# Router products in a shared buffer rotation, and the preparation steps of the second feed-forward spread over more products

## The chip, the cores and the metric

The kernel runs on one core of one Trainium2 chip, in one launch. The metric is the device time of that launch in microseconds (us); lower is better. Engines are named as in the profile: PE is TensorE's matmul, PEld its weight load, DVE is VectorE, ACT is ScalarE, POOL is GpSimd, SP is SyncE, whose queue (SPq) issues most DMAs. L670 is line 670 of the kernel.

## The reference

Two layers over x of shape (8, 512, 512), each with a gated cross-attention and a gated feed-forward. The change touches only the last of the four stages:

```python
# x: (8, 512, 512); ctx: (8, 64, 512); 32 experts, 8 groups, inner width 192
x = x + tanh(g_xattn[0]) * linear_attention(layernorm(x), ctx, ...)      # "xa0"
x = x + tanh(g_ffn[0])   * gelu_mlp(layernorm(x), ...)                   # "ff0", width 2048
x = x + tanh(g_xattn[1]) * masked_softmax_attention(layernorm(x), ctx)   # "xa1"
x = x + tanh(g_ffn[1])   * merged_moe(layernorm(x), ...)                 # "ff1"

def merged_moe(h):
    probs = softmax(h @ gate_weight.T)                  # (token, 32)
    top_val, top_idx = top_k(probs, 8)
    top_val = top_val / sum(top_val)
    w = sum over k of top_val[k] * onehot(merge_groups[top_idx[k]], 8)   # (token, 8 groups)
    gate, up = split(h @ gate_up[dominant_experts])     # 8 groups x 192 each
    y = (silu(gate) * up) @ down[dominant_experts]
    return sum over groups of w * y
```

All is float32, and all eight groups are computed for every token, weighted by w.

## The kernel before, in words

A batch of 512 tokens is the unit of the outer loops: eight batches go through the first attention, then eight through the first feed-forward (ff0), then eight through the second (ff1). Every big matrix product is done by a scheme of seven half-size products instead of eight; a "product" below is one of these seven. A product of an up projection (class Up, L754) is four matmuls of 128x128 by 256 columns, which the profile counts as eight.

In ff1 a batch has six up units (Ff1Up, in the order 1, 0, 3, 2, 5, 4) and one down projection (SplitDown, L941). The products of a unit come in the order 1, 2, 6, 5, 7, 4, 3, those of the down in the order 2, 4, 1, 6, 5, 7, 3. The last two products of an up unit, and the last of the down, are held back and issued after the first product of the next unit. So the end of a batch's 49 products reads: last unit's 2, 6, 5, 7 (38th to 41st), down 2 (42nd), last unit's 4 and 3 (43rd, 44th), down 4, 1, 6, 5, 7 (45th to 49th). SplitDown splits each of its products a second time in seven; for that `combine` (L928 to L931) forms four sums of 128x384 on DVE ("split2", "split4" and so on, two buffers in rotation) before the product that takes them.

After an up product ACT copies the result out of PSUM (u1, u6, u7, L766), DVE adds two results (g L833, up L847), ACT takes the tanh (th, L836), and DVE multiplies by the token's share of the group (L837, L839) and by the other half (a, L843 and L851). The buffers u, g, th and up are all drawn from one rotation of eight tiles of 2 KB a partition (`temp`, L121).

Beside the products of batch n runs the preparation of batch n + 1, a generator (`prep_ff1`). Each of its steps is taken after some product of the plan. In ff1 it is: second attention (transposes pt, scores pst, psc, softmax, pe, pr), layer norm and transposes again, router logits (plt, pl), the largest 8 of 32 (L657, L658), their scaling (L663), and then for each of four blocks of 128 tokens a product by group on POOL (wg_e, 128x256, L670) and a sum over experts on DVE (w, L673). Then w is transposed on PE (pw, L677), copied (wT), written to DRAM ("shares", L680, ACT's queue), and read back in five broadcast DMAs on SP's queue into the tiles "share" of the first two units (`spread_share`, L695). Last come the four token sums S (L539 to L542). The loop over the plan deals out the steps evenly: `count` steps over `until` products; the last piece (S) is taken at a given product of the down.

What sets the order: in the attention and ff0 the order on some engines is that of the code. From the first batch of ff1 on (`in_order.clear()`) no engine is held to it, and a scheduler orders each engine's instructions by the place at which the code issues them and by its own idea of when operands are ready. Each engine then executes its own queue in that order, and an instruction that waits holds all behind it. SP's queue also loads the weights, in tiles of 256 KB into a ring of 16 tiles, in the order in which the products use them.

Of the kernel before, what the change touches and what calls it, by code (L numbers as in the profile page):

```python
# [21 lines left out]
F32 = mybir.dt.float32  # L22
# [8 lines left out]
P = 128  # L31
B, S, D = 8, 512, 512
# [6 lines left out]
E, G, I = 32, 8, 192  # L39
# [29 lines left out]
def flamingo_kernel(  # L69
# [39 lines left out]
    def psum(name):  # L109
        return bank["ps"].tile([P, 512], F32, tag="ps", name=name)  # L110
# [10 lines left out]
    def temp(name):  # L121
        return work.tile([P, 512], F32, tag="t2", name=name, bufs=8)
# [406 lines left out]
    def prep_xa0(b):  # L529
        xnT = yield from normed("xa0", b, f"xa0_{b}")  # L530
        yield "last"
        blocks["xa0", b] = xnT, token_combinations("xa0", b, xnT)

    def token_combinations(ph, b, xnT):

        s = work.tile([P, 4, 2, H2], F32, tag="S", name=f"S_{ph}_{b}", bufs=1)
        a11, a12 = xnT[:, 0:2, 0:H2], xnT[:, 2:4, 0:H2]
        a21, a22 = xnT[:, 0:2, H2:S], xnT[:, 2:4, H2:S]
        nc.vector.tensor_tensor(s[:, 0], a21, a22, ALU.add)  # L539
        nc.vector.tensor_tensor(s[:, 1], s[:, 0], a11, ALU.subtract)  # L540
        nc.vector.tensor_tensor(s[:, 2], a11, a21, ALU.subtract)
        nc.vector.tensor_tensor(s[:, 3], a12, s[:, 1], ALU.subtract)  # L542
        return s

    def prep_ff0(b):
        xnT = yield from normed("ff0", b, f"ff0_{b}")

        xb = xs["ff0", b]
        for t in range(NT):
            nc.gpsimd.tensor_tensor(xb[:, t, :], xb[:, t, :], b2_sb, ALU.add)  # L550
        yield "last"
        blocks["ff0", b] = xnT, token_combinations("ff0", b, xnT)
# [74 lines left out]
    def prep_ff1(b):  # L627
        yield from cross_attention(b)
        xnT = yield from normed("ff1", b, f"ff1_{b}")

        plt = psum(f"plt_{b}")[:, 0:P]
        for c in range(NC):
            for t in range(NT):
                nc.tensor.matmul(
                    plt[ts(t, E), :],
                    lhsT=router_sb[:, c, :],
                    rhs=xnT[:, c, ts(t, P)],
                    start=c == 0,
                    stop=c == NC - 1,
                )  # L640
        lT = hpool.tile([P, P], F32, tag="lT", name=f"lT_{b}", bufs=1)
        nc.scalar.copy(lT, plt)
        yield
        pl = psum(f"pl_{b}")[:, 0 : NT * E]
        nc.tensor.transpose(pl, lT, ident)
        pl = pl.rearrange("p (t e) -> p t e", e=E)
        top = small.tile([P, NT], F32, tag="rtop", name=f"rtop_{b}")
        nc.vector.tensor_reduce(top, pl, AX.X, ALU.max, negate=True)

        pr = hpool.tile([P, NT, E], F32, tag="router", name=f"router_{b}", bufs=1)  # L650
        for t in range(NT):
            nc.scalar.activation(pr[:, t, :], pl[:, t, :], AF.Exp, bias=top[:, t : t + 1])
        yield
        best = small.tile([P, NT, 8], F32, tag="best", name=f"best_{b}")
        rest = hpool.tile([P, NT, E], F32, tag="rest", name=f"rest_{b}", bufs=1)
        for t in range(NT):
            nc.vector.max(best[:, t, :], pr[:, t, :])  # L657
            nc.vector.match_replace(rest[:, t, :], best[:, t, :], pr[:, t, :], 0.0)  # L658
        total = small.tile([P, NT], F32, tag="rtotal", name=f"rtotal_{b}")
        nc.vector.tensor_reduce(total, best, AX.X, ALU.add)  # L660
        nc.vector.reciprocal(total, total)
        nc.vector.tensor_tensor(pr, pr, rest, ALU.subtract)
        nc.vector.tensor_tensor(pr, pr, total.unsqueeze(2).to_broadcast([P, NT, E]), ALU.mult)  # L663

        wg_e = hpool.tile([P, G, E], F32, tag="wg_e", name=f"wg_e_{b}")
        w = small.tile([P, G, NT], F32, tag="w", name=f"w_{b}")
        for t in range(NT):
            if t:
                wg_e = hpool.tile([P, G, E], F32, tag="wg_e", name=f"wg_e_{b}_{t}")
            nc.gpsimd.tensor_tensor(  # L670
                wg_e, of_group, pr[:, t, :].unsqueeze(1).to_broadcast([P, G, E]), ALU.mult
            )
            nc.vector.tensor_reduce(w[:, :, t], wg_e, AX.X, ALU.add)  # L673
        for _ in range(4 if b == 0 else 2):
            yield
        pw = psum(f"pw_{b}")[0 : G * NT, 0:P]
        nc.tensor.transpose(pw, w.rearrange("p g t -> p (g t)"), ident)  # L677
        wT = hpool.tile([G * NT, P], F32, tag="wT", name=f"wT_{b}", bufs=1)
        nc.scalar.copy(wT, pw)
        nc.scalar.dma_start(out=shares[b], in_=wT)  # L680
        yield
        for i in FF1_UNITS[0:2]:
            spread_share(b, i)
        yield "last"
        blocks["ff1", b] = xnT, token_combinations("ff1", b, xnT)
# [3 lines left out]
    def spread_share(b, i):  # L689

        t = hpool.tile([P, 2, S], F32, tag="share", name=f"share_{b}_{i}", bufs=3)
        rows = shares[b].rearrange("(g t) q -> g (t q)", t=NT)
        for n in range(2):
            for g, lo, hi in pieces(P * (2 * i + n), P * (2 * i + n + 1), P):
                nc.sync.dma_start(  # L695
                    out=t[lo % P : (hi - 1) % P + 1, n, :],
                    in_=rows[g : g + 1, :].partition_broadcast(hi - lo),
                )
        spread_of[b, i] = t
# [305 lines left out]
    class QUp(Up):  # L1005
        ph, i = "xa0", 0
# [116 lines left out]
    def steps(units, late=late):  # L1123
# [9 lines left out]
    work_list = (  # L1133
        [("xa0", b, prep_xa0(b)) for b in range(B)]
        + [("ff0", b, prep_ff0(b)) for b in range(B)]
        + [("ff1", b, prep_ff1(b)) for b in range(B)]
    )

# [70 lines left out]
    for b in range(B):  # L1209
# [15 lines left out]
        g = GUp(b)  # L1225
# [50 lines left out]
    plan = []  # L1276
# [29 lines left out]
    down_of = {u.b: u for u, _, _ in plan if isinstance(u, SplitDown)}  # L1306

    def tiles_of(u, m):

        if isinstance(u, SplitDown):  # L1310
            n, of = SPLIT_ORDER.index(m), 7 * SPLIT_CHUNKS
            return -(-of * 7 // 4) - of * 6 // 4 if n == 6 else of * (n + 1) // 4 - of * n // 4
        return 1 if u.kind == "up" else u.chunks // 2
# [15 lines left out]
    hpool = stack(tc.tile_pool(name="inner", bufs=1, reuse_waits="tile"))  # L1329
# [31 lines left out]

    def steps_of(ph, b, _):

        return 5 if ph == "ff0" else 22 if b else 24

    at, held = None, False
    for u, m, n in plan:
        if n != at:
            if n == 2 * B:
                in_order.clear()  # L1370
            if at is not None and n < 3 * B:
                for _ in work_list[n][2]:
                    pass
            at, k, held = n, 0, False
        if n == 2 * B and k == 0:
            for _ in builder:
                pass
            build.close()
            second = stack(tc.tile_pool(name="second", bufs=1, reuse_waits="tile"))
        u.step(m)  # L1380
        for _ in range(tiles_of(u, m)):
            next(loads, None)
        for _ in range(4):
            if pending:
                pending.pop(0)()
        if isinstance(u, Ff1Up) and u.i == FF1_UNITS[-1]:

            if m == 2:
                down_of[u.b].combine(2)
                down_of[u.b].combine(4)  # L1390
            if m == 3:
                down_of[u.b].combine(1)
        if isinstance(u, SplitDown) and m in (4, 1, 6, 5, 7):
            u.combine(SPLIT_ORDER[SPLIT_ORDER.index(m) + 1])
        k += 1
        if k == 6:
            flush()
        if u.kind == "up" and u.ph == "ff1" and m == 5 and u.i < 4:
            spread_share(u.b, FF1_UNITS[FF1_UNITS.index(u.i) + 2])
        if k % 4 == 0:  # L1400
            next(builder, None)
        if n + 1 == 3 * B:
            continue
        if n == B + 2 and k == 10:
            groups()
        if k == 20 and n + 2 < 3 * B:
            load_x(*work_list[n + 2][0:2])
        prep = work_list[n + 1][2]
        if held:
            if u.kind == "down" and u.b == work_list[n][1] and m == u.order[1]:  # L1410
                for _ in prep:
                    pass
            continue

        until = sum(p == n for _, _, p in plan) - 6
        count = steps_of(*work_list[n + 1])
        if k * count // until > (k - 1) * count // until:
            held = next(prep, None) == "last"
# [47 lines left out]
```

## Time and profile before

| | us |
|---|---|
| median of 3 runs | 2149.47 (2148.35 to 2151.68) |
| the profiled execution | 2149.74 |
| its span | 2147.9 |
| PE waits for w before pw | 15.5 in 6 waits |
| POOL waits for w before wg_e | 15.8 in 24 waits |
| wg_e on POOL, 128x256, median | 0.727 (0.722 to 1.039), 32 of them |
| w on DVE, median | 0.421, 32 of them |
| a sum of 128x384 for the down (L928 to L931) | 0.55 |
| an elementwise 128x512 on DVE (L839) | 0.69 |

The span is the profiled execution from its first to its last instruction; its own time includes what lies around that. Durations of single instructions are those of the profile's rows; a start-to-start distance is the time that an engine was really taken up, because matmuls overlap at their ends. The batches of ff1 follow each other at 118 to 120 us in the chain of work that ended last (the down's product 4 starts at 1290.1, 1408.5, 1528.6, 1648.1, 1766.3, 1886.3, 2006.1 and 2111.5), and the last of them, with no preparation beside it, takes 105.4.

### The profile page before, as it was taken

Reading aid. Unit: us, or ns where it says so; the run is one execution under the profiler, and the core shown is the slowest. Engines: PE = TensorE matmul, PEld = TensorE weight load, DVE = VectorE, ACT = ScalarE, POOL = GpSimd, SP = SyncE. Lnnn points to the kernel's source line nnn. Section 1 sums busy time; section 2 is a strip of 40 time slices with the busy share of each in tenths; the row PEclk is TensorE's granted clock in tenths of the full one; section 3 lists DMA queues with packets and bytes.
Section 4 is the critical chain, followed back from the end, with each engine's and each line's share of the span. In section 5 each row is a group of like instructions: output and inputs, shape, how many; then the busy total and the mean of one; then the engine's idle time right before and its main releaser. Section 6 shows DMA issues by size and latency. Waiting matters only on the chain.

```text
span 2147.9 us, 30849 instructions
## 1 busy us (share of the span) xinstructions
PE 2096.3 (98%) x11452; PEld 1810.3 (84%) x11452; DVE 1241.4 (58%) x2289; ACT 557.4 (26%) x1146; POOL 251.7 (12%) x228
## 2 busy tenths in 40 slices
PE   8999999999999999999999999999999999999998
PEld 4778787788888888888888889898888889888988
DVE  3687787542333324232434377777777777776757
ACT  3433333212130303121233221312122222213121
POOL 2121111321111120030200010000000000000000
PEclk8999999999999999999999999999999999999999
DMA  7345634677676765666747658586776758585865
GB/s 221 118 152 168 198 120 111 219 243 226 203 232 181 241 205 168 200 213 189 229 156 251 193 167 284 180 265 198 233 229 199 250 169 282 166 263 158 251 205 166
DMA packets 258453, 434.84 MB, mean 202 GB/s; under 512 B 34304, under 2 KB 75936, under 8 KB 254208
## 3 DMA queue, kind: packets, MB, share of 16 engines
q1 hardware_dynamic: 250864, 406.10, 61.0%
q10 hardware_dynamic: 5856, 23.20, 2.9%
q0 software_dynamic: 1584, 3.57, 0.7%
q8 instruction: 92, 1.51, 0.3%
q14 instruction: 57, 0.47, 0.1%
HBM read 369.00 MB, written 63.77 MB: 201 GB/s over the span
## 4 chain that ended last, share of the span: by engine, by line
PE 77%; issue 7%; DVE 7%; DMA 4%; POOL 3%; SPq 1%; ACT 1%; POOLq 0%; ACTq 0%; DVEq 0%
PE x_ff L754 24%; PE w_ff L754 12%; PE x_ff_down L870 10%; PE z_ff L754 6%; PE x_ff_down L941 5%; PE w_ff_down L870 5%; PE w_ff_down L941 3%; PE z_ff_down L870 3%; PE v_ff_down L941 2%; PE pt_ff L427 1%; SPq L60 1%; PE pt_xa L427 1%; POOL wg_e L670 1%; PE pr L620 1%; PE pst L578 1%
## 5 line engine op out<-in xcount | busy, mean ns | idle before, releaser
L766 ACT COPY u_ff<-x_ff 128x512 f32<-128x512 f32 x240 | 139.8, 583 | 757.3 <-PE x_ff L754 757.1
L754 PE MATMUL w_ff<-S_ff,w_ff_up 128*128 128x256 f32 x1280 | 307.0, 383 | 0.6 <-DVE a_ff L809 0.6
L754 PE MATMUL x_ff<-S_ff,w_ff_up 128*128 128x256 f32 x1280 | 303.6, 380 | 1.8 <-ACT u_ff L766 1.8
L754 PE MATMUL x_ff<-xnT_ff,w_ff_up 128*128 128x256 f32 x1280 | 299.4, 383 | 0.0
L754 PEld LDWEIGHTS w_ff<-S_ff,w_ff_up 128*128 128x128 f32 x1280 | 242.5, 192 | 38.2 <-DMA w_ff_up<-ff_up 3.8
L754 PEld LDWEIGHTS x_ff<-S_ff,w_ff_up 128*128 128x128 f32 x1280 | 240.0, 190 | 38.0 <-issue 4.8
L754 PEld LDWEIGHTS x_ff<-xnT_ff,w_ff_up 128*128 128x128 f32 x1280 | 240.5, 191 | 37.3 <-issue 6.3
L870 PE MATMUL x_ff_down<-w_ff_down,a_ff 128*128 128x256 f32 x768 | 169.7, 379 | 0.0
L870 PEld LDWEIGHTS x_ff_down<-w_ff_down,a_ff 128*128 128x128 f32 x768 | 145.8, 190 | 19.8
L886 DVE SCALAR_TENSOR_TENSOR x_ff<-x_ff_down,gates,x_ff 128x512 f32<-128x512 f32 x32 | 24.0, 750 | 222.8 <-PE x_ff_down L870 217.2
L754 PE MATMUL z_ff<-xnT_ff,w_ff_up 128*128 128x256 f32 x640 | 151.5, 379 | 0.0
L754 PEld LDWEIGHTS z_ff<-xnT_ff,w_ff_up 128*128 128x128 f32 x640 | 119.4, 190 | 15.5 <-DMA w_ff_up<-ff_up 0.4
L870 PE MATMUL w_ff_down<-w_ff_down,s_ff 128*128 128x256 f32 x512 | 113.1, 379 | 0.0
L870 PEld LDWEIGHTS w_ff_down<-w_ff_down,s_ff 128*128 128x128 f32 x512 | 97.1, 190 | 13.1
L809 DVE TENSOR_TENSOR a_ff<-w_ff,u_ff 128x512 f32<-128x512 f32 x64 | 43.8, 685 | 92.5 <-ACT u_ff L766 90.4
L847 DVE TENSOR_TENSOR up_ff<-w_ff,u_ff 128x512 f32<-128x512 f32 x96 | 65.8, 685 | 35.2 <-ACT u_ff L766 33.4
L814 ACT ACTIVATE a_ff<-a_ff,b_sb 128x256 f32<-128x256 f32 x128 | 58.1, 501 | 93.7 <-DVE a_ff L809 93.4
L793 DVE TENSOR_TENSOR s_ff<-a_ff,a_ff 128x512 f32<-128x512 f32 x56 | 40.0, 715 | 68.1 <-ACT a_ff L814 67.9
L550 POOL TENSOR_TENSOR x_ff<-x_ff,b_sb 128x512 f32<-128x512 f32 x28 | 36.9, 1327 | 335.6 <-DVE xn_ff L420 335.6
L837 DVE SCALAR_TENSOR_TENSOR g_ff<-th_ff,x_ff 128x512 f32<-128x512 f32 x48 | 32.9, 686 | 73.9 <-ACT th_ff L836 73.9
L941 PE MATMUL x_ff_down<-w_ff_down,split_ff_down 128*128 128x128 f32 x576 | 69.3, 276 | 0.1
L941 PEld LDWEIGHTS x_ff_down<-w_ff_down,split_ff_down 128*128 128x128 f32 x576 | 66.7, 192 | 0.7 <-issue 0.7
(260 smaller groups left out, 3270.9 us busy)
## 6 DMA issues: line engine op xcount, KB each, us to landing
w_ff_up<-ff_up SPq DMA_DIRECT2D x560, 256.0 KB
w_ff_down<-stream SPq DMA_DIRECT2D x288, 256.0 KB
w_ff_down<-ff_down SPq DMA_DIRECT2D x224, 256.0 KB
x_ff<-x_ff SPq DMA_DIRECT2D x16, 1024.0 KB
share<-shares SPq DMA_DIRECT2D x64, 256.0 KB
ff_up<-build_ff_up SPq DMA_DIRECT2D x42, 256.0 KB
spread<-over SPq DMA_DIRECT2D x32, 256.0 KB
x_ff<-x_xa ACTq DMA_DIRECT2D x8, 1024.0 KB
```

Source lines behind the costliest of these rows:

```text
L427: nc.tensor.transpose(pt[:, c, :], xn[t][:, ts(c, P)], ident)
L550: nc.gpsimd.tensor_tensor(xb[:, t, :], xb[:, t, :], b2_sb, ALU.add)
L754: nc.tensor.matmul(p[:, n, :], lhsT=w[:, c, ts(n, P)], rhs=moving, **self.mark(m, 2 * n + c),)
L766: nc.scalar.copy(self.s[m], p)
L793: nc.vector.tensor_tensor(s1, a21, a22, ALU.add)
L809: nc.vector.tensor_tensor(h, p, s, ALU.add)
L814: nc.scalar.activation(h[:, n, :], p[:, n, :], AF.Gelu, bias=b1_sb[:, f : f + 1])
L837: nc.vector.scalar_tensor_tensor(g, th, 1.0, p, ALU.add, ALU.mult)
L847: nc.vector.tensor_tensor(u, p, s, ALU.add)
L870: nc.tensor.matmul(p[:, t, :], lhsT=a[:, k, ts(t, P)], rhs=w[k // 2][:, k % 2, :], **self.mark(m, 2 * k + t),)
L886: nc.vector.scalar_tensor_tensor(dst, src, GATE[self.ph], dst, ALU.mult, ALU.add)
L941: nc.tensor.matmul(p[n // 4][:, n % 4, :], lhsT=operand[k][:, c, :], rhs=w[at // 4][:, ts(at % 4, P)], start=m in self.OPENS and n % 4 == ...
```

## The change

The products by group no longer go into one buffer of their own. They are drawn from the rotation of eight, two products to a tile, so that four can be under way. The step count of the second feed-forward's preparation becomes 24 for all batches: between the sums w and the transpose pw lie four steps for every batch, where it was two for all but the first. For ff1 the steps are dealt out over two products more (`until`), and the last piece is taken at the down's fourth product (6) instead of its second (4). And of the two `combine` calls after the last unit's product 2, the one for the down's product 4 moves to the last unit's product 7.

```diff
-        wg_e = hpool.tile([P, G, E], F32, tag="wg_e", name=f"wg_e_{b}")
         w = small.tile([P, G, NT], F32, tag="w", name=f"w_{b}")
         for t in range(NT):
-            if t:
-                wg_e = hpool.tile([P, G, E], F32, tag="wg_e", name=f"wg_e_{b}_{t}")
+            if t % 2 == 0:
+                two = temp(f"wg_e_{b}_{t}").rearrange("p (t g e) -> p t g e", t=2, e=E)
+            wg_e = two[:, t % 2]
             nc.gpsimd.tensor_tensor(
                 wg_e, of_group, pr[:, t, :].unsqueeze(1).to_broadcast([P, G, E]), ALU.mult
             )
             nc.vector.tensor_reduce(w[:, :, t], wg_e, AX.X, ALU.add)
-        for _ in range(4 if b == 0 else 2):
+        for _ in range(4):
             yield
...
-        return 5 if ph == "ff0" else 22 if b else 24
+        return 5 if ph == "ff0" else 24
...
-            if m == 2:
-                down_of[u.b].combine(2)
-                down_of[u.b].combine(4)
+            if m in (2, 7):
+                down_of[u.b].combine({2: 2, 7: 4}[m])
             if m == 3:
                 down_of[u.b].combine(1)
...
         if held:
-            if u.kind == "down" and u.b == work_list[n][1] and m == u.order[1]:
+            if u.kind == "down" and u.b == work_list[n][1] and m == u.order[ahead]:
                 for _ in prep:
                     pass
             continue

-        until = sum(p == n for _, _, p in plan) - 6
+
+        ahead = 1 if n < 2 * B else 3
+        until = sum(p == n for _, _, p in plan) - 7 + ahead
         count = steps_of(*work_list[n + 1])
```

## The prediction

> **What bounds the kernel now.** I read the page's first two parts, then who waited for whom on PE, then the timeline round the longest of those waits, then busy time and clock in stretches. PE is the bound almost everywhere:
>
> ```profile
> span 2147.9 us, 30849 instructions
> PE 2096.3 (98%) x11452; PEld 1810.3 (84%) x11452; DVE 1241.4 (58%) x2289; ACT 557.4 (26%) x1146; POOL 251.7 (12%) x228
> ```
>
> So only two things can shorten it: less matmul work, or less PE time lost. The waits of PE (total us, times, longest) say where it is lost inside the body:
>
> ```profile
> PE pw L677 <- DVE w L673: 15.5, 6, 2.8
> PE pk L60 <- ACT ctxT L60: 6.7, 1, 6.7
> PE pt_xa L427 <- DVE xn_xa L420: 5.6, 6, 2.2
> ```
>
> The first row is more than half of all listed, and lies wholly in the second feed-forward: the small transpose pw waits for the group sums w. The timeline of the longest (start, duration, then in brackets the idle time before and its releaser):
>
> ```profile
> 1518.76 0.73 POOL L670 TENSOR_TENSOR wg_e<-of_group,router 128x256 f32<-128x256 f32 x1 [29.78 <-DVE router L663]
> 1519.52 0.42 DVE L673 TENSOR_REDUCE w<-wg_e 128x8 f32<-128x256 f32 x1 [0.91 <-POOL wg_e L670]
> 1520.38 0.73 POOL L670 TENSOR_TENSOR wg_e<-of_group,router 128x256 f32<-128x256 f32 x1 [0.89 <-DVE w L673]
> ...
> 1523.78 0.42 DVE L673 TENSOR_REDUCE w<-wg_e 128x8 f32<-128x256 f32 x1 [0.90 <-POOL wg_e L670]
> 1524.26 0.40 PE L677 MATMUL pw<-ident,w 128*32 128x128 f32 x1 [2.83 <-DVE w L673]
> 1524.45 1.92 PE L754 MATMUL x_ff<-xnT_ff,w_ff_up 128*128 128x256 f32 x4
> ```
>
> POOL and DVE take turns on the single wg_e buffer; four turns take 5.4 us, and pw stands in PE's queue in the middle of the last up unit's product 4. The row after pw is a second loss: four matmuls take 1.92 us, where the four before the stall took 1.03. Granted clock after each of the six stalls (the column before the last two):
>
> ```profile
> core 0: us, PE busy (x) PEld busy (x) DVE busy (x) ACT busy (x) POOL busy (x), PEclk, DMA share, GB/s
> 1405.70:1408.40 2.70, 2.70 (x14) 2.39 (x15) 0.93 (x2) 0.85 (x2) 0.00 (x0) 1.00 0.25 55
> 1524.30:1527.80 3.50, 3.50 (x11) 2.88 (x12) 0.73 (x2) 0.85 (x2) 0.00 (x0) 0.57 0.14 25
> 1643.90:1647.40 3.50, 3.50 (x11) 2.88 (x12) 0.75 (x2) 0.85 (x2) 0.00 (x0) 0.59 0.14 22
> 1763.40:1766.10 2.70, 2.70 (x14) 2.39 (x15) 0.87 (x2) 0.85 (x2) 0.00 (x0) 1.00 0.20 41
> 1881.70:1885.20 3.50, 3.48 (x10) 2.87 (x11) 1.16 (x2) 0.85 (x2) 0.00 (x0) 0.58 0.23 54
> 2001.50:2005.00 3.50, 3.46 (x10) 2.76 (x11) 0.80 (x2) 0.85 (x2) 0.00 (x0) 0.53 0.14 25
> ```
>
> After four of six, PE runs at little over half clock for 3.5 us.
>
> **The change, part by part.** The built order has the same instructions on every engine before and after (6014 rows on PE, 2257 on DVE, counted alike); only places and buffers differ.
>
> *The stall of pw.* Counting products within a batch's 49, the code issued the group products after the 38th and pw after the 42nd, with 22 steps over 43 products; with 24 steps over 45 it is the 36th and the 44th. In the built order pw now follows the last unit's product 3, and the four L673 stand on DVE ahead of L833 of the last unit, which takes the 38th product. Between lie products 6, 5, 7, 4, 3 of that unit (1.73 us each by start to start) and the down's first (4.69 us by the chain): 13.3 us. The sums are ready some 12 us early. Removed: all of 15.5 us (six waits of 2.53 to 2.83).
>
> With pw gone, what is late next on PE is split1 in the down's product 1 (below).
>
> *The clock.* 3.5 us times what is missing of the clock in the four low rows (0.43, 0.41, 0.42, 0.47) is 6.1 us. As a check, PE's busy time in the six batch periods is 117.25, 117.07, 117.45 and 117.26 where the clock fell and 115.74 and 115.57 where it did not: 6.4 us too much. The Trainium skill ("TensorE: Matmul & The Clock Gate", "Part 1: The HAM clock gate") says that the clock halves after at least one idle window of about 3.4 us, and a table there asks for no gaps over about 3 us; by that, these stalls of under 2.9 us cost nothing more and I would take 15.5. The rows show half clock right behind the stall, so I take 15.5 + 6.2 = 21.7 us.
>
> *Four products in a row on POOL.* 32 of 0.73 us stay; the turn of 1.32 us goes. The skill ("GPSIMD Engine Reference", "1. Specifications") says that POOL shares its SBUF interface with DVE and contends with DVE instructions that have two SBUF inputs. That speaks against a run of products beside busy DVE. Row: wg_e takes 0.72 to 1.04 us. So the run of four takes 2.9 us by the best and 4.2 us by the worst; I take 4.2. It matters only for what waits behind the reductions in DVE's queue: L839 and L843 of the fifth unit, and through L843's buffer the copy u6 of the last unit, which PE's product 7 awaits. Even with nothing overlapped, from pl on: top 0.29, exp 0.9, choice of eight 1.9 (as in the first batch, 1272.26 to 1274.2), products and last reduction 4.6, L839 and L843 1.3: 9.0 us. From pl to that product 7 stand six products, 10.4 us, less 0.8 for the copy: 9.6. Cost nothing, and not below nothing, since none of it is on PE's path; uncovered it would cost its overrun in each of seven batches.
>
> *Two of eight temporaries* are held for some 4 us longer than wg_e's own kilobyte was. The ones who ask next are u6 (above) and u7 of the last unit, which needs the fourth product on POOL only: 0.3 + 0.9 + 1.9 + 4.2 = 7.3 us after pl, where that copy starts 12 us after it. Nothing.
>
> *The sums of product 4 (combine) move* from the last unit's product 2 to its 7: four of 0.55 us. They are needed 2.0 us into the down's second product; D2 (4.69) and products 4 and 3 (3.5) lie between, 10 us for 2.2 us of work and about 4 us of other queued DVE work. Nothing.
>
> *Steps to the fourth down product.* S (4 x 0.68 on DVE) leaves the down product 1, where split1 and the sums of x stood behind it, and goes behind product 6's sums; it is needed by product 6 of the next batch, some 17 us later. The built order now runs product 6 directly after 1, without twelve matmuls of product 5 between. Its first matmul needs L963's read of x0. The last batch, which has no preparation, already runs 1 and 6 back to back, with no listed wait, only 4.94 instead of 4.69 us for product 1. The periods without clock loss show that same 4.94 (2.69 + 2.25 in the chain), the other four 4.72. So from 0 to 4 x 0.25 = 1.0 us; I take 0.5. A gain is excluded: product 1 is pure matmul.
>
> *Queues.* ACT's write of shares goes out some 2 us later relative to the down's product 4, and SP's five reads of it behind four more weight tiles. SP may stand for the write (1.8 to 2.6 us from issue to the first read now) with weights behind it; the ring holds 16 tiles, a down product eats 5.25 in 4.69 us, so there are 14 us in hand. The reads are needed over 25 us later. Nothing; without that ring up to 2 us a batch. DVE's queue is otherwise met above.
>
> *First batch's preparation* (beside the last down of the first feed-forward): its pw has no wait now; four reductions in a row may hold DVE 3 to 4 us, where the wait table shows no PE wait on that chain. From 0 to 1 us; I take 0.
>
> Sum against the profiled execution: 2149.74 - 15.5 - 6.2 + 0.5 = 2128.5. That execution is 0.3 above the median of 2149.47, so 2128.3.
>
> **Rivals.**
> - *The clock loss stays* (7%): it might belong to these places and not to the stall. For: two of six stalls show none. Against: the low rows start with the first matmul after the stall. 2149.5 - 15.5 + 0.5 = 2134.5.
> - *The wait moves to the down's products 1 and 6* (14%): DVE's copies of split1, split6 and the read of x0 come out late against PE, which now arrives without a pause. For: the margin at product 6 is about 0.7 us (the last batch's L963 ends at 2120.3, product 6 starts at 2121.0), and the present order fills 1.3 us there. Against: that batch does it without a wait. Price up to 1.3 us in seven batches: 2128.3 + 9 = 2137.
> - *The change does not do it* (2%): pw waits in its new place too: 2149.5.
> - *Slower* (4%): the router block ahead of L843 in DVE's queue. If it came later than worked out, product 7 stalls in each of seven batches, and the clock falls as now. It decides from 21.7 / 7 = 3.1 us of stall and clock loss a batch; slower by 0.2% (4.3 us) takes 3.7 a batch, that is some 2.7 us of stall after the 0.6 us of margin in the unoverlapped sum. At 3.5 us of stall with 1 us of clock loss: 2149.5 - 21.7 + 31.5 = 2159. Against it: th2 and the products overlap in that sum.
>
> **How the numbers follow.** The first case, 73%: 2128.3, from 2126 (nothing new, 6.4 of clock, 0.6 of spread) to 2131. A measurement can tell about 0.2%, 4.3 us. Leaving out the far ends of the second rival and the last two, the range is 2126 to 2136. Faster by over 0.2%: 73 + 7 + 14 = 94%; within: 2%; slower: 4%.
>
> **What would show it.** Right: no row pw <- w among PE's waits; clock 1.00 in all seven periods and their length about 115.7 instead of 118 to 120; POOL's wait for w gone; the four L673 before L833. Wrong: a PE wait on L843 or u6 (POOL block), on split1 or L963 (products 1 and 6), or a clock under 0.9 with no stall before it.

## The result, and the profile after

| | before | after |
|---|---|---|
| median | 2148.99 us (2148.35 to 2151.68, 4 runs) | 2123.72 us (2123.56 to 2125.65, 4 runs) |
| the profiled execution | 2149.74 | 2125.65 |
| its span | 2147.9 | 2123.8 |
| first batch's down product 4 (v) starts at | 1290.13 | 1288.74 |
| from there to the seventh batch's | 715.97 | 693.15 |
| from the seventh's to the eighth's | 105.44 | 105.56 |

The time falls to 0.9882 of before (0.9865 to 0.9899): 25.3 us, where 21.2 were forecast. 2123.7 lies under the 2128.3 of the forecast, and under the lower end of its range, 2126.

PE's busy time falls by 7.5 us (it includes the matmuls that a low clock stretched), and its instructions are the same 11452:

```profile
span 2123.8 us, 30856 instructions
PE 2088.8 (98%) x11452; PEld 1807.3 (85%) x11452; DVE 1238.9 (58%) x2289; ACT 555.4 (26%) x1146; POOL 251.5 (12%) x228
```

In PE's waits (total us, times, longest) the row of pw is gone, and what leads now lies in the first attention:

```profile
PE pt_xa L427 <- DVE xn_xa L420: 5.7, 5, 2.2
PE pk L60 <- ACT ctxT L60: 5.4, 1, 5.4
```

The same place in the timeline: POOL makes its four products in one run, the sums are ready by 1507.2, and pw comes 12.4 us later, without a bracket behind it, that is without a wait:

```profile
1502.72 3.23 POOL L670 TENSOR_TENSOR wg_e<-of_group,router 128x256 f32<-128x256 f32 x4 [19.03 <-DVE router L663]
...
1506.42 0.73 DVE L673 TENSOR_REDUCE w<-wg_e 128x8 f32<-128x256 f32 x2
...
1519.52 0.27 PE L677 MATMUL pw<-ident,w 128*32 128x128 f32 x1
```

Two whole periods of after: PE is busy for all of each, at full clock (the column before the last two):

```profile
1404.30:1519.80 115.50, 115.50 (x726) 102.46 (x725) 88.65 (x180) 28.73 (x62) 7.10 (x9) 1.00 0.73 229
1519.80:1635.30 115.50, 115.50 (x726) 102.47 (x726) 88.67 (x180) 28.73 (x62) 7.10 (x9) 1.00 0.72 229
```

All six full periods take 115.53 us; before they took 118.1 to 120.1.

### The profile page after: what moved, and what is told of

Its sections match the earlier page's. It is cut to its first block, busy times and chain, and to the rows that moved or that the text cites. A ratio compares the mean times of both kernels' runs of the same rounds, so it can differ in the third digit from the quotient of the medians.

```text
span 2123.8 us, 30856 instructions
## 1 busy us (share of the span) xinstructions
PE 2088.8 (98%) x11452; PEld 1807.3 (85%) x11452; DVE 1238.9 (58%) x2289; ACT 555.4 (26%) x1146; POOL 251.5 (12%) x228
## 3 DMA queue, kind: packets, MB, share of 16 engines
q0 software_dynamic: 1584, 3.57, 0.7%
## 4 chain that ended last, share of the span: by engine, by line
PE 82%; issue 8%; DMA 3%; DVE 3%; POOL 2%; SPq 1%; ACT 1%; POOLq 0%; ACTq 0%; DVEq 0%
PE x_ff L754 25%; PE w_ff L754 13%; PE x_ff_down L870 10%; PE z_ff L754 6%; PE x_ff_down L941 5%; PE w_ff_down L870 5%; PE w_ff_down L941 3%; PE z_ff_down L870 3%; PE v_ff_down L941 2%; PE z_ff_down L941 2%; PE pt_ff L427 1%; SPq L60 1%; PE pt_xa L427 1%; PE pr L620 1%; PE pst L578 1%
## 5 line engine op out<-in xcount | busy, mean ns | idle before, releaser
L754 PE MATMUL x_ff<-xnT_ff,w_ff_up 128*128 128x256 f32 x1280 | 293.2, 379 | 0.0
L839 DVE TENSOR_TENSOR g_ff<-g_ff,share 128x512 f32<-128x512 f32 x96 | 67.1, 699 | 2.1
```

The costliest lines, as they stand in the source:

```text
L754: nc.tensor.matmul(p[:, n, :], lhsT=w[:, c, ts(n, P)], rhs=moving, **self.mark(m, 2 * n + c),)
L839: nc.vector.tensor_tensor(g, g, share, ALU.mult)
```

## Experiments

**Theory.** The gain is the stall of pw with the half clock behind it; the rest of the change moves nothing by itself, and what exceeds the forecast is scatter in a part of the program that the change doesn't touch. **Rivals:** the clock loss belongs to certain batches and not to the stall; single parts of the change (rotation, place of S, combine) have gains or costs of their own.

A period below is the distance from one batch's down product 4 to the next batch's. Each edit is against the kernel named; medians are of 2 to 17 runs, and a median is compared only with those measured beside it on the same chip.

### Both kernels again, and two parts alone

The kernel before, unchanged:

> The kernel before, executed again. First theory (the change removed the stalls of pw and the clock loss behind them, and the missing part of the forecast is scatter of single executions in the first 100 us, which the change does not touch): six stalls of 2.5 to 2.9 us again, half clock for about 3.5 us behind three to five of them and not always the same ones, the first down's product 4 within 2 us of 1290.1, the median within 1 us of 2149. Rival (the loss of clock belongs to certain batches): the same four stalls lose it again, the other two do not.

Measured: 2149.61 us (2148.37 to 2152.05), product 4 at 1290.41, six stalls of 2.54 to 2.83 us. Five of the six lost clock, in other batches than before: the first and fourth periods' stalls, which had kept their clock, lost it, the third's kept it. The rival of the place falls.

The changed kernel, unchanged:

> The changed kernel, executed again. First theory: every batch of the second feed-forward takes 115.5 us again at clock 1.00 (from the down's product 4 of the first batch to that of the seventh 693.2 us), while the stretch ahead of the first one differs from 1288.7 by up to 2 us; the median is 2123.7 within 1 us, and the profiled execution may stand 0 to 2 us off it. Rival (the gain beyond the forecast is the change's own): the stretch ahead of the first product 4 is again 1288.7 within 0.3, and the profiled execution again stands 2 us above the median.

Measured: 2125.38 us (2124.05 to 2126.37) beside a before of 2150.67; all periods 115.53; product 4 at 1287.18, 1.6 us earlier than in the first execution. The median moved by 1.7 between the two measurements (0.7 more than expected) while the periods are the same to 0.01; and the profiled execution lies 1.3 under its median this time, where it lay 1.9 above.

Rotation alone (against before):

```diff
-        wg_e = hpool.tile([P, G, E], F32, tag="wg_e", name=f"wg_e_{b}")
...
-            if t:
-                wg_e = hpool.tile([P, G, E], F32, tag="wg_e", name=f"wg_e_{b}_{t}")
+            if t % 2 == 0:
+                two = temp(f"wg_e_{b}_{t}").rearrange("p (t g e) -> p t g e", t=2, e=E)
+            wg_e = two[:, t % 2]
```

> Before, with only the products by group drawn from the rotation, two to a tile. The turn about between POOL and DVE is gone: four products of 0.73 to 0.9 us and one reduction of 0.42 with some 0.3 of semaphores, 3.6 to 4.3 us where it was 5.4; but pw stands about 0.5 us earlier in PE's queue. So pw still stalls, by 1.3 to 1.9 us. First theory (clock is lost by a stall when it is long enough): fewer of the six lose clock, 0 to 2: 2149.0 - 6 x 1.1 - 3 to 6 = 2136 to 2140. Rival (clock is lost at that place whatever the stall): four again, 2142. Second rival (the rotation alone removes the stall): 2124 to 2128.

Measured: 2129.09 us (2128.53 to 2129.91), 0.9898 (0.9883 to 0.9913): nearest to the second rival, and 1 us above its range. No stall is left, although the code issues the products and pw where it did. The expectation missed two things that the timeline shows: the four products take 2.78 us in a run, and the scheduler put the last unit's product 7 into the middle of the down's product 2, so that PE came 0.07 us after the last sum (1517.99 + 0.42). With so little to spare the cure is partly luck:

```profile
1515.17 2.78 POOL L670 TENSOR_TENSOR wg_e<-of_group,router 128x256 f32<-128x256 f32 x4 [28.14 <-DVE router L663]
...
1517.99 0.42 DVE L673 TENSOR_REDUCE w<-wg_e 128x8 f32<-128x256 f32 x1 [0.26 <-POOL wg_e L670]
...
1518.48 0.27 PE L677 MATMUL pw<-ident,w 128*32 128x128 f32 x1
```

Its periods are 115.87 to 115.98, some 0.4 above the changed kernel's (in one period compared, 0.21 of it at up products and 0.14 at the down's).

Step count alone (against before):

```diff
-        for _ in range(4 if b == 0 else 2):
+        for _ in range(4):
...
-        return 5 if ph == "ff0" else 22 if b else 24
+        return 5 if ph == "ff0" else 24
```

> Before, with only the step count 24 and four steps between the sums w and pw; own buffer, combine and the place of S as before. First theory: pw stands behind the down's first product and the sums are issued a product or two earlier; the stall is gone or under 0.3 us, clock 1.00, and the time is that of the changed kernel, 2123.7 within 1.5; from the first batch's product 4 to the seventh's 693 to 694.5 us. Rival (the turn about on the single buffer is what hurts, or the later place of S): a stall of over 1 us or split1 late in the down's product 1 stays, 2128 to 2140.

Measured: 2129.45 us (2128.62 to 2131.68), 0.9899 (0.9884 to 0.9914). The stall and the clock loss are gone here too, but a period takes 116.05 (one of the six 116.53), which the first theory did not have; the time lies in the rival's range, but without the rival's stall. Comparing PE's starts through a period shows where: 0.41 us at the second pr of the preparation, and 0.13 at the down's products 1, 5 and 6. The first pr takes 1.06 us to the next start, the second 1.46:

```profile
1699.95 1.13 PE L620 MATMUL pr<-ctxd,eT 64*128 64x512 f32 x4
1701.01 1.99 PE L754 MATMUL x_ff<-S_ff,w_ff_up 128*128 128x256 f32 x8
1702.94 1.53 PE L620 MATMUL pr<-ctxd,eT 64*128 64x512 f32 x4
1704.40 1.78 PE L754 MATMUL w_ff<-S_ff,w_ff_up 128*128 128x256 f32 x7
```

DVE began to read the first pr (L621) only at 1702.56, behind four operations of its queue that it began after the first pr had started; that the second pr waits for a buffer of the first is inferred from this. 24 steps over 43 products leave one product between the two pr; 22 over 43, and 24 over 45, leave two. So either edit removes the stall, and the theory that the rest is worth nothing falls.

### Stall length and clock, the two further products, a sum formed twice

To the rotation-only kernel, a copy of w that pw must take, behind n more products on POOL. They add work, and their results go nowhere:

```diff
+        if b:
+            late = hpool.tile([P, G, E], F32, tag="late", name=f"late_{b}", bufs=1)
+            for _ in range([1, 2, 3, 4, 6, 8, 5][b - 1]):
+                nc.gpsimd.tensor_tensor(
+                    late, of_group, pr[:, 3, :].unsqueeze(1).to_broadcast([P, G, E]), ALU.mult
+                )
+            flat = late.rearrange("p g e -> p (g e)")[:, 0 : G * NT]
+            nc.gpsimd.tensor_copy(flat, wp)
+            wp = flat
+        nc.tensor.transpose(pw, wp, ident)
```

(The second kernel has 5, 3, 2, 4, 1, 2, 3 in the list. Lines behind the edit have higher numbers, so pw is L687.)

> The kernel with the rotation only, in which pw had no wait, plus a copy of w on POOL that pw has to take, behind 1, 2, 3, 4, 6, 8 and 5 further products by group (0.69 us each; results unused) in the seven batches: stalls of pw of some 0.69 n - 0.3 us, so in the six full periods about 1.1, 1.8, 2.5, 3.8, 5.2 and 3.2 us. First theory (the clock falls when PE idles for a large part of some fixed stretch): half clock for about 3.5 us behind 3.2, 3.8 and 5.2 in any case, behind 2.5 mostly, 1.8 sometimes, 1.1 never; time 2129 + 17.6 + 5 to 8 + up to 4 for the first batch = 2152 to 2159. Rival, the skill's rule of an idle stretch of about 3.4 us: loss behind 3.8 and 5.2 alone. Second rival (the place): loss in batches that have nothing to do with the length.

> The same with 5, 3, 2, 4, 1, 2 and 3 further products: stalls of about 1.8, 1.1, 2.5, 0.4, 1.1 and 1.8 us in the six full periods, about 3 in the batch ahead of them. First theory: loss behind 2.5 mostly, behind the two of 1.8 sometimes, behind 0.4 and 1.1 never; time 2129 + 8.7 + 3 + 1 to 5 = 2140 to 2146. Rival, the rule of 3.4 us: no loss in the six, clock 1.00. Second rival (the place): loss in the same batches as in the other kernel.

Measured: 2159.32 us, 0.3 above the expected range, and 2144.12, within it. A further product cost 0.8 us and not 0.69, so the stalls came out longer than expected. The stalls of the first kernel, in brackets:

```profile
1403.03 0.29 PE L687 MATMUL pw<-ident,late 128*32 128x128 f32 x1 [1.84 <-POOL late L685]
1521.59 0.29 PE L687 MATMUL pw<-ident,late 128*32 128x128 f32 x1 [2.60 <-POOL late L685]
1640.96 0.39 PE L687 MATMUL pw<-ident,late 128*32 128x128 f32 x1 [3.41 <-POOL late L685]
1764.60 0.39 PE L687 MATMUL pw<-ident,late 128*32 128x128 f32 x1 [5.00 <-POOL late L685]
1889.49 0.39 PE L687 MATMUL pw<-ident,late 128*32 128x128 f32 x1 [6.61 <-POOL late L685]
2011.20 0.28 PE L687 MATMUL pw<-ident,late 128*32 128x128 f32 x1 [4.21 <-POOL late L685]
```

And the 3.5 us behind each:

```profile
1403.10:1406.60 3.50, 3.50 (x17) 3.11 (x18) 1.21 (x3) 0.85 (x2) 0.00 (x0) 1.00 0.20 48
1521.70:1525.20 3.50, 3.50 (x17) 3.10 (x17) 0.85 (x2) 0.85 (x2) 0.00 (x0) 1.00 0.16 34
1641.00:1644.50 3.50, 3.50 (x9) 2.87 (x10) 0.00 (x0) 0.26 (x1) 0.00 (x0) 0.50 0.02 5
1764.70:1768.20 3.50, 3.50 (x9) 2.83 (x10) 0.00 (x0) 0.26 (x1) 0.00 (x0) 0.50 0.02 5
1889.60:1893.10 3.50, 3.50 (x10) 2.85 (x10) 0.00 (x0) 0.26 (x1) 0.00 (x0) 0.55 0.02 5
2011.30:2014.80 3.50, 3.50 (x11) 2.86 (x11) 0.00 (x0) 0.83 (x2) 0.00 (x0) 0.63 0.02 5
```

In the second kernel the stalls of 2.63, 1.80, 0.68, 1.81 and 0.97 us kept clock 1.00; 3.40 lost it, and this time 2.60 as well. Of the last of these the stall and the stretch behind it:

```profile
1994.98 0.28 PE L687 MATMUL pw<-ident,late 128*32 128x128 f32 x1 [2.60 <-POOL late L685]
```
```profile
1995.10:1998.60 3.50, 3.50 (x10) 2.80 (x10) 0.00 (x0) 0.37 (x2) 0.00 (x0) 0.55 0.02 5
```

All stalls of pw in four executions, with the two of the kernel before:

| stall, us | stalls | with clock loss |
|---|---|---|
| 0.68 to 1.84 | 5 | 0 |
| 2.53 to 2.83 | 15 | 10 |
| 3.40 to 6.61 | 5 | 5 |

At both ends the length decides: no loss under 1.9 us, a loss in every case from 3.4 us on. In the middle band the clock column shows what else counts. In the traces the clock falls and rises only at the marks of a fixed grid of 3.413 us. In the first execution of before, for example, it falls at 1523.86, 1643.33, 1882.26 and 2001.73, which lie 35, 70 and 35 steps of 3.413 apart, and it is back one step after each. Stretches of before cut at these marks, three round a stall of 2.53 us that lost clock, two round one of the same length that kept it:

```profile
1639.92:1643.33 3.41, 1.40 (x9) 0.94 (x8) 0.84 (x2) 0.48 (x1) 2.16 (x3) 1.00 0.70 227
1643.33:1646.74 3.41, 2.89 (x8) 2.36 (x9) 0.55 (x2) 0.85 (x2) 0.01 (x1) 0.50 0.02 5
1646.74:1650.15 3.41, 3.41 (x27) 3.25 (x26) 3.23 (x6) 0.00 (x0) 0.00 (x0) 1.00 0.88 187
1759.38:1762.80 3.42, 1.47 (x10) 1.01 (x8) 0.84 (x2) 0.48 (x1) 2.10 (x3) 1.00 0.73 228
1762.80:1766.21 3.41, 2.83 (x15) 2.52 (x16) 1.40 (x3) 0.85 (x2) 0.07 (x1) 1.00 0.19 41
```

PE is busy for 1.40 us of the grid step ahead of the loss, and for 1.47 us of the one that nothing follows. All 25 stalls divide in this way: each of the 15 that lost clock has 2.01 us or more of its idle time within one grid step, and the half clock begins with the next step; the 10 that kept it have at most 1.95 us in any one step. Of the two of 2.60 us, the one that kept the clock lies across a mark, with 1.69 us before it, and the other lies within one step. Elsewhere it is the same: after the first 10 us of all eighteen traces, every full-clock step with PE busy for under 42% of it is followed by half clock, and none with over 45% is. So the length and the place of the stall on the grid decide together. As an estimate from these figures, a stall of 2.54 us at a random place has 2.0 us within one step in 57% of cases (it keeps the clock only if the mark falls between 0.54 and 2.0 us into it, which is 1.46 of 3.41 us).

The rule of the Trainium skill ("TensorE: Matmul & The Clock Gate", "Part 1: The HAM clock gate"), that the clock halves after an idle window of about 3.4 us, leaves ten losses unexplained; here some 2.0 us of idle time in a step of 3.41 were enough. The section also says that the window runs freely and does not start anew with the kernel; the grid agrees with that, since the stalls lie at other places of it in each execution.

The step spread over 43 products, and S taken at the down's product 4 again (against after):

```diff
-            if u.kind == "down" and u.b == work_list[n][1] and m == u.order[ahead]:
+            if u.kind == "down" and u.b == work_list[n][1] and m == u.order[1]:
...
-        ahead = 1 if n < 2 * B else 3
-        until = sum(p == n for _, _, p in plan) - 7 + ahead
+        until = sum(p == n for _, _, p in plan) - 6
```

> The changed kernel with the 24 steps dealt out over 43 products again and S at the down's fourth-but-three product (4) as before; rotation, four steps to pw and the moved combine stay. First theory (dealing 24 steps over 43 products leaves only one product between the two pr, whose second then waits 0.4 us for DVE to release the first; the stretch to 45 takes that away): as with the step count alone, 116.05 us a period, 2128 to 2129.5. Rival (the step-only kernel was slower because of the single buffer or of the place of combine): 2124.5, as the changed kernel.

Measured: 2128.95 us (2126.04 to 2131.14), 0.9911 (0.9898 to 0.9925), periods of 116.11. The second pr loses 0.41 us here too, and the down's products 1, 5 and 6 lose 0.39 where the changed kernel loses 0.20. So the two products more and the later place of S, which look like bookkeeping, are together worth 0.58 us a period, some 3.5 in six.

The sums for the down's product 1 formed once (against after). The loop forms them after the last unit's product 3 and again after the down's product 4:

```diff
-        if isinstance(u, SplitDown) and m in (4, 1, 6, 5, 7):
+        if isinstance(u, SplitDown) and m in (1, 6, 5, 7):
```

> The changed kernel without the second of two identical calls of combine for the down's product 1 (the loop calls it after the last unit's product 3 and again after the down's product 4): four sums of 0.55 us less on DVE a batch, split1 ready some 2 us earlier. If the 0.20 us that the down's product 1 loses in every period is its wait for split1, the period falls from 115.53 to 115.3 and the time by 1.5, to about 2123. Rival (product 6's wait for the read of x0 sets it, or nothing of DVE does): periods stay at 115.53, 2124.5.

Measured: 2123.69 us beside a before of 2148.63, 0.9886 (0.9871 to 0.9901); periods of 115.32. The chain of after and then of this kernel, products 1 and 6 in one piece of 84 matmuls:

```profile
1524.48 9.58 PE x_ff_down L941 x84
```
```profile
1407.40 9.38 PE x_ff_down L941 x84
```

9.38 is twice 4.69, the time of a product without any wait. So the 0.20 us came from forming again sums that had been formed before.

### What the final kernel needs

The products in their own buffer again (the rotation's diff of above undone in after), and combine back (the sums for both products formed after the last unit's product 2):

> The changed kernel with the products by group in their own single buffer again; steps, S and combine as changed. First theory (once pw stands some 16 us behind the products, their turn about between POOL and DVE, 5.4 us instead of 3.7, hides altogether): no wait of pw, 115.53 us a period, clock 1.00, the time of the changed kernel, 2123.7 to 2125.4. Rival (the rotation is needed: four waits of 0.9 us on DVE hold up the copies and sums that PE awaits): a wait on L843 or the inner sums, periods of 116 or more, 2128 and up.

> The changed kernel with the four sums for the down's product 4 formed after the last unit's product 2 again, beside those for its product 2. First theory: PE's order is unchanged and DVE has room, 115.53 us a period, time of the changed kernel. Rival (the four sums ahead of the last unit's results hold up split2 or a copy that PE awaits): up to 0.5 us a period more, 2127 to 2128.

Measured: 2125.92 us (2125.55 to 2127.39) and 2125.90 (2124.92 to 2127.26) beside 2125.62 (2124.73 to 2128.92) for the changed kernel. With the own buffer the periods take 115.46, with combine back 115.53. Neither edit moves the periods by more than 0.07 once pw stands late. The rotation gains 0.3 us once, in the first batch's preparation: from the chain's ff0 down product at 1052 us to the first product 4 it is 237.50 us with the own buffer, as before (237.49), and 237.19 with the rotation. The 0.07 a period goes the other way, so over the whole program the rotation gains nothing that shows once pw stands late.

The kernel with split1 formed once, and the changed kernel, again:

> The changed kernel with split1 formed once, again, beside the changed kernel in the same call: periods of 115.33 us, 1.4 us under the changed kernel as a median; the stretch ahead of the first down's product 4 anywhere from 1285 to 1291. Rival (the earlier 2123.7 was scatter): no difference to the changed kernel.

> The changed kernel a third time, for the comparison with the three others: periods of 115.53 us; median 2123.5 to 2125.5; the stretch ahead of the first down's product 4 anywhere from 1285 to 1290.

Measured: 2124.47 us (2124.35 to 2124.79) and 2125.62; periods of 115.32 and 115.53, product 4 at 1289.25 and 1287.86. Forming split1 once is 1.15 us better here although the first product 4 of its profiled execution came 1.4 us later. It is the fastest kernel here; from the periods it is worth 7 x 0.2 = 1.4.

### Where the first 460 us differ

An unused buffer of one kilobyte in the place of the old one (against after, the edit below), measured twice; then the changed kernel, and the one with the step count alone, both unchanged:

> The changed kernel with an unused buffer of one kilobyte in the place of the old one for the products (one element of it is written per batch). If the place of buffers in memory costs the start: the first ff0 down's product 2 at 459 to 460.5 us and a median 2 us above the changed kernel's in this call. If it is scatter of single executions: anywhere from 455.5 to 460.5, and the medians within 1 us of each other.

> The same kernel once more: by the place of buffers 459 to 460.5 us again and 2 us above the changed kernel; by scatter a value that need not be that of the first.

```diff
+        pad = hpool.tile([P, G, E], F32, tag="wg_e", name=f"pad_{b}")
+        nc.gpsimd.tensor_copy(pad[:, 0, 0:1], of_group[:, 0, 0:1])
```

> The changed kernel, beside them: by the place of buffers 456 to 458.5 us; by scatter 455.5 to 460.5. Periods of 115.53.

> The kernel with the step count alone, which has the own buffer, again: by the place of buffers 459 to 460.5 us; by scatter 455.5 to 460.5. Periods of 116.05 in either case, so 3.6 us above the changed kernel plus what the start makes.

Measured: 2124.15, 2124.17, 2125.80 and 2128.72 us; the first ff0 down's product 2 at 457.25, 457.37, 457.32 and 457.24. The kernel with such a buffer, both times, and the one with the old buffer start as the changed kernel does, so the place of buffers isn't the cause. The medians with the unused buffer are 1.6 us under the changed kernel's, not within 1 us of it as expected for scatter, and not above it as expected for the place of buffers; this stays unexplained. In the eighteen executions profiled, the first product 4 of ff1 lies anywhere from 1285.4 to 1291.0, and the two of before are among the latest. One kernel, that with the step count alone, had its first ff0 down's product 2 at 460.30 in one execution and at 457.24 in another: scatter, whose source no run here shows.

## Why the prediction was right and wrong

**Right: the bound, the mechanism, the sign.** The wait for w is gone, the periods run at clock 1.00 and no wait took its place. The predicted time was too high by 4.6 us: 2.9 in the sum against the profiled execution (2128.5 for 2125.65), 1.9 between that execution and the median, less the 0.2 by which I had gone the same way. The step that failed, and put the time under the range, is the spread: 0.6 us were allowed, and the scatter of executions made 3.0 of the 4.6, namely the 1.9 just named and 1.1 at the start of the program (below). The rest are terms of the sum that were mis-sized: 1.0 at the stall, 0.35 at the down's product 1, 0.3 in the first batch's preparation, 0.1 at the clock. (The low end of the range, too, does not follow as written: the 0.5, 0.2 and 0.6 named for it lead from 2128.3 to 2127, and 2126 was given.)

**The stall: right in kind, its cost too small.** "Removed: all of 15.5 us" took the listed idle for the cost. That idle begins when the last matmul has drained. Before, round a stall without clock loss:

```profile
1402.05 1.03 PE L754 MATMUL x_ff<-xnT_ff,w_ff_up 128*128 128x256 f32 x4
1405.62 0.28 PE L677 MATMUL pw<-ident,w 128*32 128x128 f32 x1 [2.54 <-DVE w L673]
1405.74 1.03 PE L754 MATMUL x_ff<-xnT_ff,w_ff_up 128*128 128x256 f32 x4
1406.60 1.89 PE L754 MATMUL w_ff<-S_ff,w_ff_up 128*128 128x256 f32 x8
1408.33 2.17 PE L941 MATMUL v_ff_down<-w_ff_down,a_ff 128*128 128x128 f32 x18
```

The second four matmuls hold PE for 0.86 (1405.74 to 1406.60), the first four for their full 1.03. So a stall costs 0.17 us more than its bracket: 6 x 0.17 = 1.0 us that I left out, although I had used starts elsewhere. The stretch in after, which has the same instructions and no stall, confirms it:

```profile
1516.07 1.89 PE L754 MATMUL x_ff<-xnT_ff,w_ff_up 128*128 128x256 f32 x8
1517.79 1.89 PE L754 MATMUL w_ff<-S_ff,w_ff_up 128*128 128x256 f32 x8
1519.63 2.17 PE L941 MATMUL v_ff_down<-w_ff_down,a_ff 128*128 128x128 f32 x18
```

It takes 3.57 us before rounding (1516.07 to 1519.63), and 6.28 in before (1402.05 to 1408.33): 2.54 for the bracket and 0.17 more. One reading beside it was wrong too, without a cost: the first row of PE's waits is more than half of the three rows shown, but 15.5 of 43.3 us of all that the view lists.

**The clock: right.** 6.2 forecast. Behind the four stalls that lost clock the stretch just shown takes, less the bracket, 5.21, 5.15, 5.43 and 5.43 us, where it takes 3.74 behind the two that kept it: 6.3 in all, against the 6.4 of the check by busy time. With 15.5 and 1.0 that is the 22.8 us of the six periods. To take the rows and not the skill's 3.4 us was right: by that figure none of this would have been counted. (The table that asks for no gaps over 3 us stands further on in that page, not in Part 1.) That it was four of six hung on where the stalls lay on the grid, which the forecast did not know; another execution had five.

**The down's product 1: half right.** Forecast +0.5, with "a gain is excluded". Products 1 and 6 of after take 9.58 to 9.59 in every batch. Before they took 9.70 (4.94 + 4.76) behind a stall that kept the clock and in the first batch, and 9.47 where the clock had been low and DVE had caught up: three of each in the six periods, and a 9.47 in the last one. That is 3 x (-0.11) + 4 x 0.12 = +0.15. What I had for a loss by the new order is the late split1, and a gain was possible, since twelve matmuls of product 5 between 1 and 6 had cost 0.07. I also didn't see why S had to move: left in its old place, with the 24 steps over 43 products, it costs 0.58 a period (the second pr and the down together).

**POOL's run, temporaries, combine, queues: nothing, as forecast.** The run took 3.23 us, inside the 2.9 to 4.2. **First batch:** I took 0 with nothing below it; the rotation saved 0.3. **Before that**, 1.1 us are scatter of the start.

So 15.5 + 1.0 + 6.3 - 0.15 + 0.3 + 1.1 = 24.05 for 24.1 us of span.

**The median and the range.** I gave 0.6 us of spread, from three runs of before. The changed kernel's sixteen runs in four measurements have a median of 2125.5 (2123.6 to 2128.9), the 66 of before 2149.7 (2145.1 to 2154.3); the four runs first shown were at the low end of their kernel. Against these longer medians the gain is 24.2 us and the forecast 2.8 too high, and 2125.5 still lies 0.5 under the range. The range should have gone some 2 us lower for single executions alone.

**Still open:** what moves the first 460 us.

## What to carry to other kernels

Cost a stall on PE by the distance of starts, not by the listed idle, and add the slower clock behind it: none showed here below 1.9 us, in all five cases from 3.4 us on, and between 2.5 and 2.9 us it depended on whether 2.0 us of the stall fell into one step of the clock's grid. There, reckon with a chance and widen the range for it. A stall can have several sufficient cures (a wider rotation, or more steps between sums and transpose); look at which of them is really needed, and at what the new spacing does elsewhere, as with the two pr. And a small loss that recurs in every period at full load is worth tracing to its operand: here to sums that were formed twice.

## What the runs showed of the hardware that was not expected

- Stalls of 2.53 to 2.83 us halved PE's clock in 10 of 15 cases, shorter ones (0.68 to 1.84) in 0 of 5, longer ones (3.40 to 6.61) in 5 of 5. The clock changed only at the marks of a grid of 3.413 us, and fell when 2.01 us or more of a stall lay within one step (15 of 15), not with 1.95 or less (0 of 10).
- One loss in the two executions of before added 1.3 to 1.7 us behind the stall. Behind the stalls of 3.41 and 5.00 us the clock stayed low for two steps, and the period grew by 2.9 and 2.3 us beyond the stall.
- A product of 128x256 on POOL took 0.69 us in one run of four (2.78), 0.81 in a run of four beside a busier DVE (3.23; DVE was busy for 2.38 us of it, and for 1.27 of the 2.78), 0.8 in the longer runs of the stall experiments. That DVE is the cause was not tested.
- The first 460 us, in which PE, DVE and ACT had the same instructions in the same order in all eighteen executions, varied by 5 us from one execution to another (455.5 to 460.3 at the first ff0 down's product 2), and by 3 us between two of one kernel (460.30 and 457.24).
